# Expert rows turned by transposing DMAs as 16-bit halves, in place of TensorE transposes

## The chip, the cores and the metric

The kernel runs on one core of one Trainium2 chip. The metric is the device time of one execution in microseconds (us), as the median of several runs. The engines are called PE or TensorE (matmuls; PEld is its weight load), DVE or VectorE, ACT or ScalarE, POOL or GpSimd, and SP, which here only issues DMAs. DMAs that SP issues go through hardware queue q1, the gathers that GpSimd issues go through software queue q0; both are served by the same 16 DMA engines.

## The reference

Two layers of "cross attention" and feed-forward work on `x` of shape [4, 512, 512], 2048 tokens of 512 numbers in all. Each part adds its result to `x`:

```python
x = x + L0_xattn(ctx, layernorm(x))   # a state-space scan
x = x + L0_ffn(layernorm(x))          # mixture of 64 experts, 8 for each token
x = x + L1_xattn(layernorm(x), ctx)   # 16 heads of attention
x = x + L1_ffn(layernorm(x))          # two ternary matrix products with GELU between
```

The change lies in the second part, the mixture of experts:

```python
# the gate chooses 8 of 64 experts for each token; rare choices are rerouted
flat_e = rerouted.reshape(-1)
order = jnp.argsort(flat_e)
tok = order // TOP_K
xs = x[tok]                                         # rows sorted by expert
gu = ragged_dot(xs, swapaxes(gate_up_proj, 1, 2), group_sizes)   # [rows, 2*192]
gate, up = split(gu, 2)
y = ragged_dot(silu(gate) * up, swapaxes(down_proj, 1, 2), group_sizes)
out = zeros_like(x).at[tok].add(y * w[:, None])
```

So each expert takes some 230 to 350 normalised rows of 512 float32 numbers, multiplies them with a [512, 384] matrix, and the result with a [192, 512] matrix.

## The kernel before

The kernel goes through four stages in order: the scan (to about 510 us), the gate and the routing (to about 640), the experts (to about 1338), and attention with the last feed-forward (to the end). In the first three stages and in attention the instructions of each engine stand in the order in which the code issues them, so what is issued earlier on an engine or on a DMA queue also runs earlier there.

**The gate.** `Gate.norm(t)` normalises tile t (128 tokens) on ScalarE into a `g_xn` buffer (three of them, pool `r_p3`) and SP stores it to the DRAM table `xn_dram`. TensorE turns the same tile (`turn`), ScalarE copies it (`take`), and TensorE makes the logits for two tiles at a time. `exps` lets GpSimd fill the last columns of `g_z` with constants (two memsets for each tile) and `top` finds the eight best on VectorE. The order of these calls is written out in `route`; norms run four and five tiles ahead. GpSimd also computes the statistics (`Stats.pair`, lines 154 to 157) and issues loads for later keys (lines 864 to 873). The routing then makes, for each expert, a list of its tokens (`tok`).

**The experts.** `Experts.run_in` loops over i from 0 to 65. In iteration i:

- GpSimd issues indirect gathers: the rows of expert i+2 (`xg`, up to three tiles of at most 128 rows) and its weights (`wg`, 6144 bytes a partition; `wd`, 4096 bytes a partition). Buffers come from pool `e_w` with four of each name.
- For m = 0, 1, 2: TensorE does `gate_up` of expert i-1 for the m-th block of 128 outputs (`pg`, line 1314), ScalarE and VectorE make `sg` and `h` of it, and then `turn_x` turns tile m of expert i: four TensorE transposes into the PSUM tile `pt` (line 1298) and one copy to `xT` (line 1301; VectorE for tile 1, ScalarE for the others).
- TensorE does `down` of expert i-2 (`po`, lines 1338 to 1348), ScalarE and VectorE copy the result to `yo`, and SP stores it to `y_dram`.
- Side tasks of the routing and of the later feed-forward (`Ternary.tasks`) are done after that by a quota; the latter load 32 blocks of 512 KB (`wf`) through SP and reduce or round them. They fall mostly on experts 30 to 53.

`xT` has two buffers, `pg` and `po` three each. ROOM fixes how many rows each of the 64 places has, from 352 down to 232; the first 40 have three tiles, the rest two. An expert with more rows than its place would leave rows to a loop in `rest`, which runs only if there are any.

**A transposing DMA elsewhere.** In the attention stage the kernel already turns 2-byte matrices with `nc.sync.dma_start_transpose` (line 2018): `Th<-hq`, 128 by 1024 bf16, and `Tx<-xq`, 128 by 512.

Of the kernel before, what the change touches and what calls it, by code (L numbers as in the profile page):

```python
# [17 lines left out]
F32 = mybir.dt.float32  # L18
F16 = mybir.dt.float16
BF16 = mybir.dt.bfloat16  # L20
I16 = mybir.dt.int16
# [8 lines left out]
P = 128  # L30
B, S, DM = 4, 512, 512
NT = B * S // P
NC = DM // P
# [4 lines left out]
E, TOPK, SEL, FI = 64, 8, 4, 192  # L38
# [12 lines left out]
ROOM = [next(m for m, end in ROOMS if i < end) for i in range(E)]  # L51
BASE = [2 * i + min(i, THREE) for i in range(E + 1)]
# [107 lines left out]
class Gate:  # L160
# [16 lines left out]
    def norm(self, t):  # L177
        nc = self.nc
        n, i = divmod(t, 2)
        xn = self.s[t] = self.rows.tile([P, DM], F32, name="g_xn")  # L180
        nc.scalar.activation(xn, self.x_all[:, t, :], AF.Identity,
                             bias=self.stats.nmr[n][:, i:i + 1],
                             scale=self.stats.rstd[n][:, i:i + 1])
        nc.sync.dma_start(self.dr["xn"][t * P:(t + 1) * P, :], xn)

    def turn(self, t):
        xn = self.s[t]
# [997 lines left out]
class Keys:  # L1185
# [14 lines left out]
    def load(self, h0, h1, pool, tag, queue=None):  # L1200

        t = pool.tile([P, self.KC, (h1 - h0) * HD], F32, name="k_w", tag=tag)
        for h in range(h0, h1, HG):
            cols = slice(h * HD, min(h + HG, h1) * HD)
            (queue or self.nc.sync).dma_start(t[:, :, cols.start - h0 * HD:cols.stop - h0 * HD],
                                   self.w["Wk"][:, cols].rearrange("(k p) e -> p k e", p=P))
        for h in range(h0, h1):
            self.wk[h] = t[:, :, (h - h0) * HD:(h - h0 + 1) * HD]
# [40 lines left out]
        self.pss = None  # L1249


def gather(nc, pool, name, width, table, index):
    n = index.shape[0]
    t = pool.tile([P, width], F32, name=name)
    nc.gpsimd.indirect_dma_start(out=t[0:n, :], out_offset=None, in_=table,  # L1255
                                 in_offset=bass.IndirectOffsetOnAxis(ap=index, axis=0))
    return t


class Expert:  # L1260
# [3 lines left out]
    def __init__(self, cm, wp, sp, yp, ps, pg, po, w, xn_dram):  # L1264
        self.cm, self.nc = cm, cm.nc
        self.wp, self.sp, self.yp, self.ps, self.pg, self.po = wp, sp, yp, ps, pg, po
        self.w, self.xn_dram = w, xn_dram

    def load(self, widx, toks):
        s = {}  # L1270
        self.load_rows(s, toks)
        self.load_weights(s, widx)
        return s

    def load_rows(self, s, toks):

        s["n"] = [t.shape[0] for t in toks]
        s["xg"] = [gather(self.nc, self.wp, f"xg{min(j, 1)}", DM, self.xn_dram[:, :], t)
                   for j, t in enumerate(toks)]

    def load_weights(self, s, widx):
# [6 lines left out]
    def turn_x(self, s, j):  # L1288

        nc = self.nc  # L1290
        if j >= len(s["n"]):
            return
        if j == 0:
            s["xT"] = self.sp.tile([P, NC, 3 * P], F32, name="xT")
        n = s["n"][j]
        pt = self.ps.tile([P, NC, P], F32, name="pt")
        for c in range(NC):
            nc.tensor.transpose(pt[:, c, 0:n], s["xg"][j][0:n, c * P:(c + 1) * P],  # L1298
                                self.cm.ident[0:n, 0:n])
        out = s["xT"][:, :, j * P:j * P + n]  # L1300
        (nc.vector.tensor_copy if j == 1 else nc.scalar.copy)(out, pt[:, :, 0:n])  # L1301

    def gate_up(self, s, m):

# [58 lines left out]
class Experts:  # L1363
# [11 lines left out]

    def load_rows(self, i):
        if i < E:
            self.ex.load_rows(self.st[i], [
                self.r["tok"][0:min(P, ROOM[i] - j * P), j, i:i + 1]
                for j in range(BASE[i + 1] - BASE[i])])  # L1380

    def run(self, tern, more, late, keys, kv):

# [4 lines left out]
    def run_in(self, ctx, tern, more, late, keys, kv):  # L1388
        cm, ex, st = self.cm, self.ex, self.st
        tc = cm.tc  # L1390
        ex.sp = ctx.enter_context(tc.tile_pool(name="e_s", bufs=2))
        ex.yp = ctx.enter_context(tc.tile_pool(name="e_y", bufs=3))
        ex.ps = ctx.enter_context(tc.tile_pool(name="e_ps", bufs=2, space=PSUM))
        ex.pg = ctx.enter_context(tc.tile_pool(name="e_pg", bufs=3, space=PSUM))
        ex.po = ctx.enter_context(tc.tile_pool(name="e_po", bufs=3, space=PSUM))
        tp = ctx.enter_context(tc.tile_pool(name="e_t", bufs=2))
        ctx_k = late_contexts(keys, self.w, late)
        slots, norms = slot_tasks(cm, self.dr, kv, self.r, more, ex.ps)
        tasks = slots + tern.tasks(tp, ex.ps) + norms
        many = len(tasks)  # L1400
        done = 0
        held = []
        QUOTA = 54
        self.load_rows(0)
        self.load_rows(1)
        for i in range(E + 2):
            self.load_rows(i + 2)
            self.load_weights(i + 2)
            for m in range(3):
                if 1 <= i <= E:  # L1410
                    ex.gate_up(st[i - 1], m)
                if m == 0 and held:
                    held.pop()()
                if i < E:
                    ex.turn_x(st[i], m)
            if i >= 2:
                ends = list(range(ROWS[i - 2], ROWS[i - 1], P)) + [ROWS[i - 1]]
                ex.down(st[i - 2], [self.y_dram[r0:r1, :] for r0, r1 in zip(ends, ends[1:])])
                while tasks and not held and done < (i - 1) * many / QUOTA:
                    left = tasks.pop(0)()  # L1420
                    done += 1
                    if left is not None:
                        held.append(left)
        assert not tasks and not held
        return ctx_k


def late_contexts(keys, w, late):

    ctx = {}  # L1430
    for b, tag in ((2, "Th"), (3, "hq")):
        ctx[b] = late.tile([P, CTX // P, S], F32, name="k_ctx", tag=tag)
        keys.nc.sync.dma_start(ctx[b], w["ctxT"][:, b * S:(b + 1) * S].rearrange(
            "(k p) s -> p k s", p=P))
    return ctx


def slot_tasks(cm, dr, kv, r, pool, ps):
# [127 lines left out]
    def key_norms(step):  # L1566
# [9 lines left out]
        else:  # L1576
# [6 lines left out]
            for c0, c1 in cols:  # L1583
# [15 lines left out]
def rest(ctx, cm, x_all, w, xn_dram, z_dram, r, many):  # L1599


    tc, nc = cm.tc, cm.nc
# [18 lines left out]
    tok = cp.tile([P, NOV], I32, name="o_tok")  # L1621
    widx = cp.tile([P, NOV], I32, name="o_widx")
    with tc.tile_pool(name="o_ps", bufs=1, space=PSUM) as ps:
        ends = []
        for name, op in (("before", ALU.is_gt), ("upto", ALU.is_ge)):
            m = cp.tile([E, E], F32, name=f"o_{name}")
# [87 lines left out]
    wp = ctx.enter_context(tc.tile_pool(name="o_w", bufs=1))  # L1714
    ps = ctx.enter_context(tc.tile_pool(name="o_eps", bufs=1, space=PSUM))
    pg = ctx.enter_context(tc.tile_pool(name="o_pg", bufs=3, space=PSUM))
    ex = Expert(cm, wp, wp, wp, ps, pg, ps, w, xn_dram)
    with tc.For_i(0, many, 1) as i:
        at = wp.tile([P, 2], I32, name="o_at")
        vec.tensor_copy(at[:, 0:1], tok[:, bass.ds(i, 1)])  # L1720
        vec.tensor_copy(at[:, 1:2], widx[:, bass.ds(i, 1)])
        s = ex.load(at[:, 1:2], [at[:, 0:1]])
        ex.turn_x(s, 0)
        for m in range(3):
            ex.gate_up(s, m)
        ex.down(s, [z_dram[bass.ds(i * P, P), :]])
# [684 lines left out]
```

## Time and profile before

| What | us |
|---|---|
| median of 3 runs | 2589.12 (2588.2 to 2590.96) |
| the profiled execution | 2588.76 |
| its span | 2587.0 |
| experts, first `pg` matmul to first `pg` matmul of the last expert | 648.5 to 1323.5 |

| Engine | busy us (share of the span) | instructions |
|---|---|---|
| TensorE | 2452.8 (95%) | 9831 |
| VectorE | 1494.9 (58%) | 2565 |
| ScalarE | 1206.2 (47%) | 2323 |
| GpSimd | 1178.2 (46%) | 1108 |

The span is the time from the first to the last instruction of one profiled execution, and the durations of instructions are from that execution. A busy time is the union of the instructions of an engine. The DMA share is the sum of the packets' times over the time of 16 engines; it can go a little over 1, since packets of different queues overlap on an engine. A row of a wait names who waited, for whom, how long in total, how many times, and the longest one.

### The profile page before, as it was taken

Reading aid. Unit: us, or ns where it says so; the run is one execution under the profiler, and the core shown is the slowest. Engines: PE = TensorE matmul, PEld = TensorE weight load, DVE = VectorE, ACT = ScalarE, POOL = GpSimd, SP = SyncE. Lnnn points to the kernel's source line nnn. Section 1 sums busy time; section 2 is a strip of 40 time slices with the busy share of each in tenths; the row PEclk is TensorE's granted clock in tenths of the full one; section 3 lists DMA queues with packets and bytes.
Section 4 is the critical chain, followed back from the end, with each engine's and each line's share of the span. In section 5 each row is a group of like instructions: output and inputs, shape, how many; then the busy total and the mean of one; then the engine's idle time right before and its main releaser. Section 6 shows DMA issues by size and latency. Waiting matters only on the chain. (4 is left out here: it accounts for less than half of the span.)

```text
span 2587.0 us, 29356 instructions
## 1 busy us (share of the span) xinstructions
PE 2452.8 (95%) x9831; PEld 1380.1 (53%) x9831; DVE 1494.9 (58%) x2565; ACT 1206.2 (47%) x2323; POOL 1178.2 (46%) x1108
## 2 busy tenths in 40 slices
PE   6989899988999999999998999999999999999997
PEld 3555555645556566666664444445454454555543
DVE  6999998945332433444225555466665666554546
ACT  6777777655222222333223543454454445554543
POOL 7999999921443444444325333134423343121112
PEclk8999999988999999999998999999999999999999
DMA  5362535343776667899755543233433443332210
GB/s 203 95 223 89 200 127 187 103 150 113 229 221 203 217 219 258 278 334 342 232 177 189 183 130 104 80 122 110 121 104 105 134 144 100 96 96 64 69 41 21
DMA packets 226781, 401.90 MB, mean 155 GB/s; under 512 B 62163, under 2 KB 103203, under 8 KB 222528
## 3 DMA queue, kind: packets, MB, share of 16 engines
q1 hardware_dynamic: 183166, 243.57, 28.8%
q0 software_dynamic: 41408, 156.20, 19.3%
q8 instruction: 81, 1.33, 0.2%
q10 hardware_dynamic: 2050, 0.18, 0.1%
q14 instruction: 76, 0.62, 0.1%
HBM read 312.18 MB, written 79.82 MB: 152 GB/s over the span
## 5 line engine op out<-in xcount | busy, mean ns | idle before, releaser
L1956 DVE TENSOR_REDUCE mx<-psc 128x1 f32<-128x512 f32 x256 | 176.5, 690 | 408.1 <-PE psc L1953 407.9
L1314 PE MATMUL pg<-xT,wg 128*128 128x284 f32 (+12 forms) x1536 | 394.4, 400 | 1.2 <-ACT xT L1301 1.1
L1959 ACT ACTIVATE e<-psc,mx 128x512 f32<-128x512 f32 x256 | 176.0, 688 | 326.9 <-DVE mx L1956 326.3
L1314 PEld LDWEIGHTS pg<-xT,wg 128*128 128x128 f32 x1536 | 278.9, 191 | 91.1 <-issue 40.2
L492 POOL TENSOR_TENSOR dBu<-bb,du 128x1024 f32<-128x1024 f32 x128 | 303.1, 2389 | 4.7 <-DVE dA L517 3.2
L1255 POOL DMA_INDIRECT xg<-xn_dram,tok x168 | 173.0, 1030 | 203.7 <-PE pt L1298 146.3
L1953 PE MATMUL psc<-kT,qT 128*128 128x512 f32 x512 | 261.7, 593 | 0.0
L1980 PE MATMUL po<-eT,v 128*128 128x512 f32 x512 | 231.6, 595 | 9.3 <-ACT eT L1974 9.3
L1919 PE MATMUL pq<-Wq,xnT 128*128 128x512 f32 x512 | 233.5, 599 | 6.3 <-DMA Wq<-Wq 6.3
L1989 PE MATMUL px<-Wo,oT 128*128 128x512 f32 x512 | 231.9, 596 | 0.0
L1973 PEld LDWEIGHTS pet<-ident,e 128*128 128x128 f32 x1024 | 126.3, 141 | 146.6 <-issue 129.6
L1930 POOL TENSOR_SCALAR qms<-qms 128x4 f32<-128x4 f32 x64 | 24.9, 389 | 389.0 <-DVE qms L1928 388.1
L503 ACT ACTIVATE dA<-delta,negA 128x512 f32<-128x512 f32 x256 | 176.3, 694 | 53.8 <-DVE hc L518 35.0
L517 DVE TENSOR_TENSOR_SCAN dA<-dA,dBu 128x1024 f32<-128x1024 f32 x80 | 186.5, 2331 | 16.3 <-ACT dA L503 6.6
L1980 PEld LDWEIGHTS po<-eT,v 128*128 128x128 f32 x512 | 96.1, 190 | 136.1 <-issue 114.8
L1973 PE MATMUL pet<-ident,e 128*128 128x128 f32 x1024 | 154.8, 274 | 6.5 <-DVE e L1965 6.2
L1359 DVE COPY yo<-po 128x512 f32<-128x512 f32 x68 | 46.9, 690 | 196.4 <-PE po L1348 196.4
L523 PEld LDWEIGHTS yT<-ident,hc 128*128 128x128 f32 x1024 | 118.6, 143 | 77.9 <-issue 45.4
L1965 DVE TENSOR_SCALAR e<-e,tot 128x512 f32<-128x512 f32 x256 | 152.8, 597 | 9.1
L523 PE MATMUL yT<-ident,hc 128*128 128x128 f32 x1024 | 132.6, 277 | 21.0 <-DVE yg L557 9.8
L1974 ACT COPY eT<-pet 128x512 f32<-128x512 f32 x256 | 148.0, 578 | 3.2 <-PE pet L1973 2.8
L1919 PEld LDWEIGHTS pq<-Wq,xnT 128*128 128x128 f32 x512 | 93.7, 192 | 101.8 <-issue 95.4
(359 smaller groups left out, 4260.4 us busy)
## 6 DMA issues: line engine op xcount, KB each, us to landing
y_dram<-yo SPq DMA_DIRECT2D x110, 256.0 KB
bb<-bc_dram SPq DMA_DIRECT2D x16, 1024.0 KB
cb<-bc_dram SPq DMA_DIRECT2D x16, 1024.0 KB
v_dram<-v SPq DMA_DIRECT2D x64, 256.0 KB
k_dram<-k_kT SPq DMA_DIRECT2D x64, 256.0 KB
Wq<-Wq SPq DMA_DIRECT2D x16, 1024.0 KB
kT<-k_dram SPq DMA_DIRECT2D x64, 256.0 KB
rk<-r_dram SPq DMA_DIRECT2D x64, 256.0 KB
```

Of the source, the lines that this page charges most:

```text
L492: nc.gpsimd.tensor_tensor(dBus[q], st[b]["bb"][i // 2][:, j:j + 2, :], st[b]["du"][c].unsqueeze(1).to_broadcast([P, 2, S]), ALU.mult)
L503: nc.scalar.activation(dAs[q][:, j, :], st[b]["delta"][c], AF.Exp, scale=negA[:, c, n:n + 1])
L517: nc.vector.tensor_tensor_scan(*flat, 0.0, ALU.mult, ALU.add)
L523: nc.tensor.matmul(yT[:, lc, :], t[:, lc * P:(lc + 1) * P], cm.ident, is_transpose=True, start=first and lc == 0, stop=last, skip_group_ch ...
L1314: nc.tensor.matmul(pg[:, 0:n], s["wg"][:, c, m * P:(m + 1) * P], s["xT"][:, c, 0:n], start=c == 0, stop=c == NC - 1)
L1919: nc.tensor.matmul(pq.rearrange("p h d -> p (h d)"), xnTs[b * NC + i][:, c, :], s["Wq"][:, c, :], start=c == 0, stop=c == NC - 1)
L1953: nc.tensor.matmul(pscore, st[b, g]["qT"][:, h, i * P:(i + 1) * P], ks[n], start=True, stop=True)
L1956: nc.vector.tensor_reduce(mx, pscore, AX.X, ALU.max, negate=True)
L1959: nc.scalar.activation(e, pscore, AF.Exp, bias=mx, accum_out=tot)
L1973: nc.tensor.transpose(pt[:, kc, :], e[:, kc * P:(kc + 1) * P], cm.ident)
L1980: nc.tensor.matmul(po, v[:, kc, :], eT[:, kc, :], start=kc == 0, stop=kc == KB - 1)
L1989: nc.tensor.matmul(px, oTs[j * HG + h][:, i * P:(i + 1) * P], st[b, g]["Wo"][:, h, :], start=h == 0, stop=h == HG - 1)
```

## The change

The gate no longer stores a row as 512 float32 numbers. GpSimd splits each number into its low and its high 16 bits (two copies for each tile of 128 tokens) and the row is stored as 512 low halves followed by 512 high halves; the table has the same number of bytes. The gathers fetch those rows into buffers of a pool of their own (`e_x`, two of each of three names), with the number of rows rounded up to a multiple of 16.

Behind the gather, `turn_rows` issues on SP one transposing DMA for each tile, [rows x 1024] to `xt` [128 x 8 x rows] in 16-bit elements; there is one `xt` buffer for each tile number (`e_xt`). Tile m of expert i+1 is turned in iteration i. `join_x` then puts the halves together: VectorE copies the high halves and ScalarE the low ones into every second 16-bit place of `xT`, which is float32 again. `gate_up` and `down` are as before. The loop in `rest` joins the halves first and turns on TensorE as before.

```diff
@@ Gate.norm
-        nc.sync.dma_start(self.dr["xn"][t * P:(t + 1) * P, :], xn)
+        halves = xn[:, :].bitcast(I16).rearrange("p (d two) -> p two d", two=2)
+        t2 = self.work.tile([P, 2, DM], I16, name="g_halves")
+        for k in range(2):
+            nc.gpsimd.tensor_copy(t2[:, k], halves[:, k])
+        nc.sync.dma_start(self.dr["xn"][t * P:(t + 1) * P, :], t2.rearrange("p k d -> p (k d)"))
@@ Expert
+    def load_rows(self, s, toks, n):
+
+        s["n"] = n
+        s["xg"] = [gather(self.nc, self.xp, f"xg{j}", 2 * DM, self.xn_dram[:, :], t, I16)
                    for j, t in enumerate(toks)]
...
+    def turn_rows(self, s, j):
+
+        if j >= len(s["n"]):
+            return
+        n = -(-s["n"][j] // 16) * 16
+        t = self.tp.tile([P, 2 * NC, n], I16, name=f"xt{j}",
+                         padded_shape=[P, 2 * NC, P if j < 2 else 3 * P // 4])
+        self.nc.sync.dma_start_transpose(t, s["xg"][j][0:n, :])
+        s["xt", j] = t
+
+    def join_x(self, s, j):
 
         nc = self.nc
         if j >= len(s["n"]):
             return
         if j == 0:
             s["xT"] = self.sp.tile([P, NC, 3 * P], F32, name="xT")
-        n = s["n"][j]
+        n, t = s["n"][j], s.pop(("xt", j))
+        out = s["xT"][:, :, :].bitcast(I16).rearrange("p c (t two) -> p two c t", two=2)
+        at = slice(j * P, j * P + n)
+        nc.vector.tensor_copy(out[:, 1, :, at], t[:, NC:, 0:n])
+        nc.scalar.copy(out[:, 0, :, at], t[:, 0:NC, 0:n])
...
-        pt = self.ps.tile([P, NC, P], F32, name="pt")
-        for c in range(NC):
-            nc.tensor.transpose(pt[:, c, 0:n], s["xg"][j][0:n, c * P:(c + 1) * P],
-                                self.cm.ident[0:n, 0:n])
-        out = s["xT"][:, :, j * P:j * P + n]
-        (nc.vector.tensor_copy if j == 1 else nc.scalar.copy)(out, pt[:, :, 0:n])
@@ Experts.run_in
+        ex.xp = ctx.enter_context(tc.tile_pool(name="e_x", bufs=2))
+        ex.tp = ctx.enter_context(tc.tile_pool(name="e_xt", bufs=1))
...
         self.load_rows(0)
         self.load_rows(1)
+        for j in range(3):
+            self.turn_rows(0, j)
         for i in range(E + 2):
             self.load_rows(i + 2)
             self.load_weights(i + 2)
@@ in the loop over m, behind gate_up of expert i-1
                 if i < E:
-                    ex.turn_x(st[i], m)
+                    ex.join_x(st[i], m)
+                self.turn_rows(i + 1, m)
@@ whole
-    dr = dict(xn=dp.tile([B * S, DM], F32, name="xn_dram"),
+    dr = dict(xn=dp.tile([B * S, 2 * DM], I16, name="xn_dram"),
```

More of the change, by code (lines that the diff above doesn't have):

```diff
@@ L1249, in take, with gather @@
         self.pss = None
-def gather(nc, pool, name, width, table, index):
+def gather(nc, pool, name, width, table, index, dtype=F32):
     n = index.shape[0]
-    t = pool.tile([P, width], F32, name=name)
+    t = pool.tile([P, width], dtype, name=name)
     nc.gpsimd.indirect_dma_start(out=t[0:n, :], out_offset=None, in_=table,
@@ L1266, in __init__ @@
         self.wp, self.sp, self.yp, self.ps, self.pg, self.po = wp, sp, yp, ps, pg, po
-        self.w, self.xn_dram = w, xn_dram
+        self.w, self.xn_dram, self.xp = w, xn_dram, wp
     def load(self, widx, toks):
         s = {}
-        self.load_rows(s, toks)
+        self.load_rows(s, toks, [t.shape[0] for t in toks])
         self.load_weights(s, widx)
         return s
-    def load_rows(self, s, toks):
-        s["n"] = [t.shape[0] for t in toks]
-        s["xg"] = [gather(self.nc, self.wp, f"xg{min(j, 1)}", DM, self.xn_dram[:, :], t)
+    def load_rows(self, s, toks, n):
+        s["n"] = n
+        s["xg"] = [gather(self.nc, self.xp, f"xg{j}", 2 * DM, self.xn_dram[:, :], t, I16)
                    for j, t in enumerate(toks)]
@@ L1286, in load_weights @@
             "p (j h) -> p j h", j=2)
-    def turn_x(self, s, j):
+    def turn_rows(self, s, j):
[7 more added lines that the diff above has]
+    def join_x(self, s, j):
         nc = self.nc
@@ L1294, in turn_x @@
             s["xT"] = self.sp.tile([P, NC, 3 * P], F32, name="xT")
-        n = s["n"][j]
+        n, t = s["n"][j], s.pop(("xt", j))
[3 more added lines that the diff above has]
+        nc.scalar.copy(out[:, 0, :, at], t[:, 0:NC, 0:n])
+    def turn_x(self, s):
+        nc = self.nc
+        s["xT"] = self.sp.tile([P, NC, 3 * P], F32, name="xT")
+        x = self.sp.tile([P, DM], F32, name="xj")
+        out = x[:, :].bitcast(I16).rearrange("p (d two) -> p two d", two=2)
+        for k in range(2):
+            nc.vector.tensor_copy(out[:, k], s["xg"][0][:, k * DM:(k + 1) * DM])
         pt = self.ps.tile([P, NC, P], F32, name="pt")
         for c in range(NC):
-            nc.tensor.transpose(pt[:, c, 0:n], s["xg"][j][0:n, c * P:(c + 1) * P],
-                                self.cm.ident[0:n, 0:n])
-        out = s["xT"][:, :, j * P:j * P + n]
-        (nc.vector.tensor_copy if j == 1 else nc.scalar.copy)(out, pt[:, :, 0:n])
+            nc.tensor.transpose(pt[:, c, :], x[:, c * P:(c + 1) * P], self.cm.ident)
+        nc.scalar.copy(s["xT"][:, :, 0:P], pt)
     def gate_up(self, s, m):
@@ L1377, in load_rows, with turn_rows @@
         if i < E:
-            self.ex.load_rows(self.st[i], [
-                self.r["tok"][0:min(P, ROOM[i] - j * P), j, i:i + 1]
-                for j in range(BASE[i + 1] - BASE[i])])
+            n = [min(P, ROOM[i] - j * P) for j in range(BASE[i + 1] - BASE[i])]
+            self.ex.load_rows(self.st[i], [self.r["tok"][0:-(-m // 16) * 16, j, i:i + 1]
+                                           for j, m in enumerate(n)], n)
+    def turn_rows(self, i, j):
+        if i < E:
+            self.ex.turn_rows(self.st[i], j)
     def run(self, tern, more, late, keys, kv):
@@ L1722, in rest @@
         s = ex.load(at[:, 1:2], [at[:, 0:1]])
-        ex.turn_x(s, 0)
+        ex.turn_x(s)
         for m in range(3):
```

## The prediction

> **What bounds the kernel now.** I began with the page's busy times, then took the expert stage alone: the table by stretches, the timeline of one expert, and the DMA view.
>
> ```profile
> PE 2452.8 (95%) x9831; PEld 1380.1 (53%) x9831; DVE 1494.9 (58%) x2565; ACT 1206.2 (47%) x2323; POOL 1178.2 (46%) x1108
> ```
>
> The table by stretches, for experts 1 to 29, 30 to 39, 40 to 53 and 54 to 62:
>
> ```profile
> core 0: us, PE busy (x) PEld busy (x) DVE busy (x) ACT busy (x) POOL busy (x), PEclk, DMA share, GB/s
> 660.16:1002.42 342.26, 342.26 (x1547) 205.55 (x1547) 129.31 (x258) 87.40 (x205) 150.83 (x148) 1.00 0.68 214
> 1002.42:1111.80 109.38, 108.40 (x521) 67.62 (x519) 43.92 (x71) 32.36 (x74) 46.21 (x47) 1.00 0.87 292
> 1111.80:1238.69 126.89, 126.46 (x573) 88.50 (x571) 56.80 (x91) 43.05 (x83) 56.69 (x56) 1.00 0.97 333
> 1238.69:1323.46 84.77, 79.72 (x364) 57.84 (x362) 21.55 (x41) 23.56 (x50) 27.79 (x29) 0.96 0.66 211
> ```
>
> TensorE fills nearly every microsecond at full clock, so what leaves it is gain. But the last two columns say what comes next: the DMA engines are busy 0.68 of the first stretch and 0.97 of the third, where the weights of the later feed-forward pass through as well (`wf`). The change puts its work there.
>
> One expert of 284 rows in the timeline (first column start, second length):
>
> ```profile
> 902.22 2.18 PE L1314 MATMUL pg<-xT,wg 128*128 128x284 f32 x8
> 904.24 0.60 PE L1298 MATMUL pt<-ident,xg 128*128 128x128 f32 x4
> 904.67 2.08 PE L1314 MATMUL pg<-xT,wg 128*128 128x284 f32 x8
> ...
> 909.03 0.43 PE L1298 MATMUL pt<-ident,xg 28*128 28x28 f32 x4
> 909.40 0.70 PE L1338 MATMUL po<-wd,h 128*128 128x512 f32 x1
> ```
>
> From start to start the transposes take 904.67 - 904.24 = 0.43 us, again 0.43 for the second tile, and 909.40 - 909.03 = 0.37 for the short one: 1.23 us of the 11.25 us until the next expert. An expert of two tiles spends 0.85. (Modelled ends overlap; starts are the safer measure.) The overflow loop in `rest`, which keeps transposes on TensorE, did not run in this trace: 672 `pt` transposes are just 4 for each of the 168 tiles of the 64 experts. Its edit costs nothing here.
>
> **The change, part by part.**
>
> TensorE loses all 672 transposes. That is worth at most 1.25 x 29 = 36 us in the first stretch, 1.23 x 10 = 12, 0.85 x 14 = 12 and 0.8 x 9 = 7: some 67 us.
>
> Their work goes to 168 transposing DMAs on SP, each of a [128 rows x 1024 halves] tile or a part of it. The trace has exactly this operation: `Th<-hq`, 128x1024 in 2-byte elements. The DMA view of one of them alone (1888.4 to 1890.0 us, 40 slices of 0.04 us), then one that was disturbed (1820.1 to 1824.1, slices of 0.1 us):
>
> ```profile
> DMA  0002589999999999999999999999999999742100
> q1 hardware_dynamic: 1056, 0.26, 85.4%
> ...
> DMA  0000000000071799999990000000000599999025
> GB/s 0 0 0 0 0 0 0 0 0 0 0 164 31 151 210 218 192 215 177 69 23 0 0 13 5 10 10 10 8 10 10 118 282 289 287 318 418 20 61 205
> ```
>
> Alone it takes 85.4% of 1.6 us = 1.4 us of all 16 engines, 190 GB/s, in packets under 512 B. Disturbed, everything stands for about 1 us in the middle while only some 10 GB/s trickle, and the tile takes 2.5 us from first packet to last. It looks as if the engines move in step in such a transfer and wait for the slowest. In the expert stage gathers are under way nearly always; no row shows a transpose beside a gather. So a tile costs between 1.4 and 2.7 us; I take 1.8, nearer to the quiet row, because an engine that waits may serve another queue.
>
> What the other transfers need: 214 GB/s x 342.26 us / 29 = 2.53 MB an expert, then 3.19, 3.02 and 1.99 MB. The fastest five microseconds of this stage moved
>
> ```profile
> 1214.00:1219.00 5.00, 5.00 (x27) 4.17 (x26) 1.45 (x2) 1.73 (x3) 2.75 (x3) 1.00 1.04 401
> ```
>
> 401 GB/s, so those are 6.3, 8.0, 7.5 and 5.0 us an expert. An expert has 2.25, 2.125, 2 and 1.9 tiles. The period is the larger of TensorE's new time and the DMA sum (us an expert):
>
> - experts 1 to 29: before 11.80, TensorE after 10.55; DMA 6.3 + 4.05 = 10.35. Gain 1.25 x 29 = 36.
> - 30 to 39: before 10.94, TensorE 9.71; DMA 8.0 + 3.8 = 11.8. Loss 9.
> - 40 to 53: before 9.06, TensorE 8.2; DMA 7.5 + 3.6 = 11.1. Loss 2.04 x 14 = 29.
> - 54 to 62: before 8.6 (a stall of 7 us at one of them left aside), TensorE 7.8; DMA 8.4. Gain 2.
>
> Sum: 0. At 1.4 us a tile DMA needs 9.45, 11.0, 10.3 and 7.6: -36, +1, +17, -7 = -25 us. At 2.7 us, 12.4, 13.7, 12.9 and 10.1: +17, +28, +54, +14 = +113.
>
> Here the Trainium skill speaks for the change: "Advanced Engine Details and Errata", section "X-Bar Transpose (TRN2)", expects a transposing DMA at 350 to 400 GB/s, as fast as a copy. Then a tile of 262 kB is about 0.7 us, TensorE stays the bound nearly everywhere, and the sum is -36 -12 -2 -7 = -57. The row says 1.4, half that rate; the row decides. Another rule speaks against: "VectorE: DVE Perf Modes", section "The three transpose paths", gives 1309 ns for one 128x128 block by DMA and advises TensorE where PSUM will do. Eight such blocks one after another would be 10.5 us a tile, over 20 us an expert; the row has eight in 1.4, so as a rate it does not hold.
>
> Waits on SP. `turn_rows(i+1, m)` waits for its gather and for both joins of expert i (one `xt` buffer each). Behind it stand the `y_dram` stores and the `wf` loads. An issue takes 1.24 us (`Th` group): 3 x 1.24 plus the four stores (903.04 to 905.89, 2.85 us) is 6.6 of 10 us, and SP waited 529 us for `yo` before; no cost while landings come within about 8 us, which is when the next expert's join wants the tile. POOL's row gathers, which waited 146 us for TensorE, now wait for a transpose that landed an iteration earlier: hidden.
>
> Joins: ScalarE copied 104 tiles out of PSUM (583 ns), VectorE 64 (692). Now both copy half of all 168; nearest row the 128x512 VectorE pass at 597 ns. Both engines are at most 45% busy in every stretch, and a joined tile is first used an iteration later: cost 0, unless the tile lands late; then the joins hold up `sg` and `h` behind them.
>
> The gate stage. `norm` gets two GpSimd copies a tile and its store waits for them. Rows:
>
> ```profile
> L1804 POOL TENSOR_SCALAR hq<-hid 128x512 bf16<-128x512 f32 x64 | 44.0, 705 | 166.0 <-DVE hid L1803 166.0
> ...
> 530.07 0.23 POOL L157 TENSOR_SCALAR s_all<-s_all 128x2 f32<-128x2 f32 x1
> 530.23 0.10 POOL L219 MEMSET g_z<- 128x4 f32 x1
> ...
> DVE g_z L230 <- POOL g_z L219: 4.7, 2, 4.1
> ```
>
> GpSimd is late already: VectorE waits 4.1 us for that first memset. In the order of instructions the copies of tiles 0 to 4 come between L157 and it: 10 x 0.7 = 7 us, and about 2 us because two `g_halves` buffers wait for stores to land. ScalarE's fourth normalisation, at 518.9, also waits for a `g_xn` buffer that GpSimd reads only after 530. Later the copies fit (2.8 us in a pair's 7). Cost 9 us, all on the path to the first gather; 5 if a copy takes 0.35 us, 14 at the 1.28 of a two-operand pass.
>
> The start of the stage. SP first issues the two `k_ctx` loads, then the transposes of expert 0:
>
> ```profile
> 645.13 3.58 SPq L1433 DMA_DIRECT2D k_ctx<-ctxT  x2
> ...
> 648.53 5.06 PE L1314 MATMUL pg<-xT,wg 128*128 128x352 f32 x8 [0.57 <-ACT xT L1301]
> ```
>
> 1 MB at the 250 to 290 GB/s of these microseconds is 4 us in the same queue, then three transposes (5) and a join (0.6): near 657 in place of 648.5. Cost 8 us (4 to 14).
>
> Sum: 0 + 9 + 8 = +17 us. The profiled execution took 2588.8 us (span 2587.0), 0.4 below the median of the runs, 2589.1; so 2589 + 17 = 2606 us. A measurement here can tell about 0.2%, 5 us, from no change.
>
> **Rivals.**
>
> 1. Transposes are cheap beside gathers (quiet row or the skill's rate). For: the dense stretch already ran at 97% without stalling TensorE. Against: the disturbed row. Time: -25 + 17 = -8, to -57 + 17 = -40: 2581 to 2549, less if the gate costs only 5. This is the faster side; it decides where a tile costs under 1.5 us.
> 2. Transposes in step hold all engines (2.7 us a tile): +113 + 17, 2719. For: the disturbed row; gathers have packets of 4 and 6 KB. Against: it was seen with other traffic in the same queue only.
> 3. Landing latency: with one buffer each, turn, landing and join form a ring; over 8 us, joins hold ScalarE and SP. One more microsecond in each of the 33 experts of the later stretches: +33 on the sum, 2639. SP's long waits for `yo` speak against it in the first stretch.
>
> That the change doesn't do what it says is unlikely: the order of instructions has no `pt` transposes for the 64 experts and 168 DMAs instead.
>
> **How the numbers follow.** The sum as taken (2590 to 2640): 0.38. Rival 1: 0.31. Rival 2: 0.12. Rival 3: 0.12. Within 5 us by cancellation: 0.07. The range 2562 to 2690 leaves out the far halves of rivals 1 and 2. Faster 0.31, same 0.08, slower 0.61.
>
> **What would show it.** Right: by stretch, periods near 10.5 in experts 16 to 23 (before 11.25) but over 10 in 40 to 53 (before 9.0), with DMA share near 1 and ScalarE or VectorE waiting for `xt`; the first `g_z` memset 9 us later; the first `pg` matmul 8 us later relative to its first gather. Wrong: TensorE still without gaps in 40 to 53 (rival 1), or periods over 11.5 already in the first stretch (rival 2).

## The result, and the profile after

The changed kernel takes 2788.3 us (median of four runs, 2782.97 to 2817.36) where the kernel before, on the same chip, takes 2588.66 (2584.45 to 2590.96): a ratio of 1.0796 with a 95% interval of 1.0720 to 1.0872, 200 us slower. The prediction said 2606, with a range to 2690.

The profiled execution took 2782.97 us (span 2781.3), against 2588.76 (2587.0) before: 194 us more. The page's line of busy times:

```profile
PE 2438.8 (88%) x9159; PEld 1363.4 (49%) x9159; DVE 1519.6 (55%) x2669; ACT 1269.3 (46%) x2387; POOL 1187.4 (43%) x1140
```

TensorE issues the 672 transposes less, as planned (9159 matmuls for 9831), yet its busy time falls by only 14 us, and its share from 95% to 88%. The table by stretches shows where; these are the same experts as in the prediction's table (1 to 29, 30 to 39, 40 to 53, 54 to 62):

```profile
core 0: us, PE busy (x) PEld busy (x) DVE busy (x) ACT busy (x) POOL busy (x), PEclk, DMA share, GB/s
682.65:1042.52 359.87, 320.02 (x1199) 187.19 (x1199) 140.51 (x316) 116.14 (x234) 143.39 (x146) 0.94 1.11 250
1042.52:1206.91 164.39, 110.26 (x402) 67.81 (x402) 47.01 (x90) 42.02 (x84) 44.34 (x48) 0.82 1.11 227
1206.91:1404.28 197.37, 135.24 (x458) 92.72 (x458) 59.56 (x106) 56.29 (x98) 54.31 (x56) 0.81 1.12 250
1404.28:1511.79 107.51, 79.65 (x291) 56.77 (x291) 23.65 (x51) 31.40 (x60) 29.33 (x31) 0.84 1.07 226
```

The stretches are 17.6, 55.0, 70.5 and 22.7 us longer than before, 166 us together. In each, two columns contradict each other: the DMA share is over 1, but the bytes moved are 226 to 250 GB/s, where the same engines moved 292 and 333 GB/s in the second and third stretch before. Something keeps the DMA engines occupied without moving data. TensorE's granted clock (PEclk) fell too, from 1.00 to 0.81 in the third stretch.

Who waits for it, from the waits of the changed kernel (who waited, for whom, us in total, times, longest):

```profile
POOL xg L1259 <- DMA xt<-xg: 450.3, 95, 18.2
DVE xT L1312 <- DMA xt<-xg: 311.5, 85, 17.0
ACT xT L1313 <- DMA xt<-xg: 307.1, 90, 17.0
PE pg L1339 <- ACT xT L1313: 171.4, 33, 13.8
ACT yo L1384 <- DMA y_dram<-yo: 68.3, 31, 5.0
```

Line 1299 is now the transposing DMA (`xt<-xg`), 1312 and 1313 the two joins, 1339 `gate_up`, 1384 a copy to `yo`. TensorE's share of these waits is the row with 171 us, behind ScalarE's join, which in turn waits for the turned tile.

One stall, from the timeline (start, length, engine):

```profile
1172.12 8.59 SPq L1299 DMA_TRANSPOSE xt<-xg  x2
...
1187.33 0.76 ACT L1313 COPY xT<-xt 128x512 int16<-128x512 int16 x1 [6.06 <-DMA xt<-xg]
...
1189.30 0.41 ACT L1350 COPY h<-h 64x264 f32<-64x264 f32 x1
...
1190.10 8.41 PE L1339 MATMUL pg<-xT,wg 128*128 128x264 f32 x24 [6.79 <-ACT h L1350]
```

SP needs 8.59 us to issue two transposing DMAs (over the whole kernel the median of one issue is 1.93 us and the longest 13.52; the fields are min, median and max in ns):

```profile
L1299 SPq DMA_TRANSPOSE xt<-xg x168: 846/1926/13520, 656.0 to 1501.2; - x168
```

The tile lands at 1187.33; ScalarE sat 6.06 us ahead of its join, with `sg` and `h` of the expert before queued behind it, and TensorE stood 6.79 us. The DMA view of 1174 to 1184 us (40 slices of 0.25 us; a packet counts wholly in the slice in which it starts) shows what the DMA engines did while the two were issued and just after:

```profile
DMA  8799799990100019999969979934459123899999
GB/s 328 301 278 229 287 133 197 88 52 0 16 0 16 17 20 51 176 86 90 114 73 349 156 79 198 102 71 84 77 70 135 69 90 153 244 306 310 360 356 364
```

From 1176.25 to 1177.75 the view is dark: hardly a packet starts and 0 to 20 GB/s flow. The engines are not idle then: the packet records have 21 packets under way at 1177.0. Some of those that began before and do not end, as a plain table:

```
start us   took ns   bytes   queue      end us
1174.68      3066      256   q1        1177.75
1174.98      2760      256   q1        1177.74
1175.25      2496      256   q1        1177.75
1175.77      1982      256   q1        1177.75
1175.92      1838     4096   q0        1177.76
```

In all, 17 packets of transposing DMAs, four of them shown, stand there; they start between 1173.40 and 1175.90. Twelve end within 40 ns of 1177.76 and the other five within 15 ns of 1177.94. A packet of 256 bytes otherwise takes 18 ns (the median). They look as if they waited for one another. A packet of q0 that started behind them ends with them; but three others of q0 begin and end while they stand, and two end 0.5 us later, so q0 is slowed rather than shut.

The dark spell is only a part of this wait. From 1182.5 to 1186.5 the packets of q0 that start carry 1.12 MB, some 280 GB/s, and only 412 packets of transposing DMAs start beside them; in the last microsecond, when q0 is nearly empty, 597 do. So the tile also waited while the engines moved other data.

Over the whole expert stage the transposing DMAs have 4089 packets longer than 200 ns: 3% of their packets and 38% of their time, and three quarters of these (75%) end within 20 ns of at least three others of them. Were each end moved at random by up to 1 us, 4% would.

### The profile page after: what moved, and what is told of

Same layout as the page of the kernel before. It is cut to its first block, busy times and chain, and to the rows that moved or that the text cites. A ratio compares the mean times of both kernels' runs of the same rounds, so it can differ in the third digit from the quotient of the medians.

```text
span 2781.3 us, 28648 instructions
## 1 busy us (share of the span) xinstructions
PE 2438.8 (88%) x9159; PEld 1363.4 (49%) x9159; DVE 1519.6 (55%) x2669; ACT 1269.3 (46%) x2387; POOL 1187.4 (43%) x1140
## 5 line engine op out<-in xcount | busy, mean ns | idle before, releaser
L1339 PE MATMUL pg<-xT,wg 128*128 128x284 f32 (+12 forms) x1536 | 435.5, 447 | 197.8 <-ACT xT L1313 171.4
L1339 PEld LDWEIGHTS pg<-xT,wg 128*128 128x128 f32 x1536 | 329.9, 219 | 318.8 <-ACT xT L1313 184.9
L1259 POOL DMA_INDIRECT xg<-xn_dram,tok x168 | 162.7, 968 | 509.7 <-DMA xt<-xg 450.3
L1313 ACT COPY xT<-xt 128x512 int16<-128x512 int16 (+3 forms) x168 | 110.4, 657 | 311.2 <-DMA xt<-xg 307.1
L1312 DVE COPY xT<-xt 128x512 int16<-128x512 int16 (+3 forms) x168 | 68.6, 408 | 314.6 <-DMA xt<-xg 311.5
```

The source lines that it names most:

```text
L1339: nc.tensor.matmul(pg[:, 0:n], s["wg"][:, c, m * P:(m + 1) * P], s["xT"][:, c, 0:n], start=c == 0, stop=c == NC - 1)
```

## The experiments

Three theories stand against each other. **A, held in step:** a transposing DMA needs all 16 engines together, so that it and whatever runs beside it hold each other up, and the engines lose capacity. **B, the ring:** the DMA engines are well, and the chain of turn, landing and join through single `xt` buffers costs the time. **C, the bytes:** 37 MB more in 256-byte pieces are simply too much, transposed or not. The table gathers what the packet records say of each (expert stage, first `pg` of expert 0 to first `pg` of expert 63; packet means in ns; the 256-byte packets are those of the transposing or copying DMA; "engine time" is the sum of the packets' times over 16 engines, in us).

| Kernel | median us | ratio to before (95%) | stage us | 256 B, mean | 256 B, engine time | gathers of 4 and 6 KB, engine time |
|---|---|---|---|---|---|---|
| before | 2588.66 | | 674.9 | | | 364 |
| after | 2788.3 | 1.0796 (1.0720 to 1.0872) | 847.0 | 37 | 324 | 451 |
| 1 before + unused turns | 2738.31 | 1.0593 (1.0529 to 1.0658) | 825.8 | 35 | 314 | 418 |
| 2 before + unused plain copies | 2611.44 | 1.0114 (1.0069 to 1.0158) | 697.8 | 20 | 182 | 358 |
| 3 after, joins don't wait | 2808.12 | 1.0863 (1.0795 to 1.0931) | 887.0 | 39 | 346 | 463 |
| 4 after, plain copies | 2588.72 | 1.0018 (0.9992 to 1.0045) | 654.1 | 20 | 181 | 338 |
| 5 after, no weight gathers | 2564.5 | 0.9915 (0.9880 to 0.9951) | 636.9 | 27 | 241 | 163 |
| 6 after, weights in q1 | 2676.38 | 1.0356 (1.0324 to 1.0388) | 744.7 | 28 | 241 | 377 |
| 7 gate alone, join late | 2923.38 | 1.1311 (1.1260 to 1.1362) | 995.7 | | | 377 |
| 8 gate alone, join ahead | 2601.88 | 1.0045 (1.0024 to 1.0066) | 676.5 | | | 352 |
| 9 after, DMAs kept apart | 2733.96 | 1.0552 (1.0511 to 1.0592) | 794.3 | 26 | 225 | 328 |
| 10 before + a third of the turns | 2659.56 | 1.0264 (1.0176 to 1.0353) | 728.5 | 38 | 161 | 388 |
| 11 as 1, stores by ScalarE | 2847.32 | 1.0993 (1.0926 to 1.1061) | 938.2 | 39 | 346 | 443 |
| 12 after, stores by ScalarE | 2820.44 | 1.0889 (1.0831 to 1.0948) | 889.8 | 42 | 367 | 424 |

(The "gathers" of 6 are its weight loads in q1, with the `wf` packets of 4 KB among them, and the row gathers in q0; those of 5 are without most weights. A packet's time includes what it waits for others, so a column is occupation, not work.)

**1. The DMAs without the rest of the change.** To the kernel before, behind `turn_x`:

```diff
                     ex.turn_x(st[i], m)
+                self.unused(i + 1, m)   # dma_start_transpose(xt, xg as int16), nobody reads xt
```

> The kernel before, with TensorE's transposes and float32 rows as they were, plus the 168 transposing DMAs of the change at the same places of SP's queue, into xt buffers that nobody reads (and the row gathers in the change's two-buffer pool). The gate is untouched. Three theories of the 200 us. A (held in step): a transposing DMA needs all 16 DMA engines together, so it and the gathers beside it hold each other up, and gathers and stores come late whoever waits for the turned tile: 2700 to 2780. B (ring): what costs is the chain turn, landing, join with single xt buffers, in which ScalarE, VectorE and SP wait; nobody waits here, so 2590 to 2620. C (bytes): the 37 MB more in 256-byte pieces fill the engines, transposed or not: as A, 2700 to 2780.

Measured: 2738.31, 155 us above the runs of before beside it (2583.63). No join waits for a tile here and TensorE still has its own transposes, so B in the form of the joins' waits falls as the main cause. (The gathers still wait until a transposing DMA has read their buffer; run 2 has the same buffers.) What waits is ScalarE, for the stores to free `yo`, and the gathers:

```profile
ACT yo L1359 <- DMA y_dram<-yo: 230.2, 29, 15.7
POOL xg L1255 <- DMA xt<-xg: 224.1, 46, 16.0
```

The loss is not spread evenly: experts 16 to 29 kept the 11.25 and 11.07 us of before exactly, experts 1 to 15 went from 12.4 to 15.2 us each and 40 to 53 from 9.1 to 14.5. In experts 16 to 29 the packets are held too (a mean of 29 ns in 16 to 23 and of 36 in 24 to 29, with a DMA share of 1.07 and 1.11), with weight gathers beside them, and it costs no time. So neither a held packet nor a share over 1 is a loss by itself; it is one where TensorE runs out of work.

**2. The same bytes, plainly copied.** The rows are not turned, and nobody reads them.

```diff
-        self.cm.nc.sync.dma_start_transpose(t, x)
+        self.cm.nc.sync.dma_start(t[0:n, :, 0:P], x.rearrange("p (c k) -> p c k", c=2 * NC))
```

> As the run before it, but each of the 168 unused DMAs is a plain copy of the same bytes from xg to xt, in pieces of 256 bytes like the transposing one, rows not turned. A: a plain copy needs no step, so 2590 to 2630. B: 2590 to 2620. C: the same bytes in the same pieces, so as long as with transposing DMAs, 2700 to 2780.

Measured: 2611.44, 28 us above before, against 155. The packets have the same size and number; they take a mean of 20 ns, and not one of 144640 took over 200. So of the 155 us some 28 belong to the bytes (C, a part of it) and 127 to the transposing (A).

**3. The ring without its wait.** The joins copy a constant, so this kernel leaves out the rows.

```diff
-        nc.vector.tensor_copy(out[:, 1, :, at], t[:, NC:, 0:n])
-        nc.scalar.copy(out[:, 0, :, at], t[:, 0:NC, 0:n])
+        nc.vector.tensor_copy(out[:, 1, :, at], constant)
+        nc.scalar.copy(out[:, 0, :, at], constant)
```

> The changed kernel with its transposing DMAs, but join_x copies one constant into xT instead of the halves in xt, so that no engine waits for a turned tile to land; only the next transposing DMA into the same buffer does. A: gathers and SP's queue are still held up, 2720 to 2780. B: most of the 172 us of the expert stage come back, 2600 to 2640. C: 2720 to 2780.

Measured: 2808.12. Nothing comes back, the stage is even 40 us longer than in the changed kernel. So the joins' 311 and 307 us of waiting are where the loss shows, not what makes it. One thing did move: from the first row gather to the first `pg` it took 7.1 us, where the changed kernel takes 18.8.

**4. The ring with a plain copy in it.** The rows reach the joins, but not turned.

```diff
-        self.nc.sync.dma_start_transpose(t, s["xg"][j][0:n, :])
+        self.nc.sync.dma_start(t[0:n], s["xg"][j][0:n, :].rearrange("p (c k) -> p c k", c=2 * NC))
```

> The changed kernel with the whole ring as it is (single xt buffers, joins that wait), but the DMA between xg and xt is a plain copy in 256-byte pieces in place of a transposing one; rows are not turned. A: the loss in the expert stage goes, and TensorE is without its transposes: 2540 to 2620. B: the ring is the same, 2740 to 2790. C: 2740 to 2790.

Measured: 2588.72, as fast as before (0.9992 to 1.0045). All 200 us go when the DMA no longer transposes, with ring, joins, gate and queue order untouched. That the DMA transposes is the cause; how it does the harm, in step as A has it, this run does not show. SP's issue of one such DMA also falls, to a median of 0.61 us. The stretches of this kernel, for the same experts:

```profile
679.49:983.97 304.48, 302.97 (x1199) 176.59 (x1199) 139.21 (x316) 113.97 (x234) 151.72 (x145) 0.99 1.04 302
983.97:1092.35 108.38, 98.20 (x405) 60.10 (x403) 46.45 (x90) 41.81 (x84) 43.61 (x46) 0.97 1.04 330
1092.35:1236.44 144.09, 124.79 (x458) 84.92 (x458) 59.74 (x106) 55.55 (x98) 53.59 (x56) 0.92 1.06 347
1236.44:1322.50 86.06, 74.23 (x291) 52.90 (x291) 23.91 (x51) 31.30 (x60) 29.29 (x31) 0.92 0.94 272
```

A DMA share over 1 here goes with 302 to 347 GB/s. Against before, the stretches change by -37.8, -1.0, +17.2 and +1.3 us.

**5. Less to collide with.** From the fifth expert on, weights of the first four are used again, so this kernel leaves out 60 experts' weight gathers:

```diff
+                s["wg"], s["wd"] = self.st[i % 4]["wg"], self.st[i % 4]["wd"]
```

> The changed kernel without the weight gathers from the fifth expert on (the weights of the first four are used again), so that transposing DMAs meet only row gathers, stores and the later layer's weight loads. A: with little to hold them up, 256-byte packets fall from a mean of 37 ns towards the 20 ns of a plain copy, TensorE is the bound in experts 16 to 29 (about 9.8 us each, as with plain copies), and the kernel takes 2530 to 2600. Were a transposing DMA slow by itself (fixed 2.3 us a tile), the mean stays near 37 ns.

Measured: 2564.5. Experts 16 to 23, which meet only row gathers and stores, are bound by TensorE (9.82 us each, against 11.25 before and 12.19 in the changed kernel), and their transposing packets have means of 21 to 24 ns. SP's issue has a median of 1.24 us, as in the quiet stage. The table by stretches for them:

```profile
855.00:934.00 79.00, 79.00 (x323) 46.73 (x322) 39.97 (x70) 30.51 (x65) 23.30 (x26) 1.00 0.72 181
```

TensorE fills all 79 us, with the transposing DMAs under way. From expert 30 on, where the later layer's `wf` loads pass, stalls come back (14.66 us at expert 35, 12.45 at 49). So a transposing DMA isn't slow by itself; it becomes slow in company (which, as run 1 shows, need not cost time).

**6. The company moved to the same queue.** The loads take their weights at fixed places, and not those that the routing chose; the bytes are the same.

```diff
+                self.cm.nc.sync.dma_start(wg, self.w["gate_up"][i * P:(i + 1) * P, :])
+                self.cm.nc.sync.dma_start(wd, self.w["down"][i * P:(i + 1) * P, :])
```

> The changed kernel with the weights of experts 5 to 64 as plain loads at fixed places, issued by SP into q1 in front of the transposing DMAs: the same bytes and packet sizes, but in the queue of the transposing DMAs in place of the software queue q0. If what hurts is the meeting of two queues on an engine (A, narrow form), 256-byte packets take about 20 ns and the kernel 2540 to 2640. If any traffic beside a transposing DMA hurts (A, wide form), or plain bytes (C), it stays at 2700 to 2800.

Measured: 2676.38, between the two expectations. Over half of the loss goes when the weights stand in one queue with the transposing DMAs, and the mean falls from 37 to 28 ns. The rest stays, with row gathers still in q0. What remains is close to full engines: the packets' times of the five largest kinds sum to 734 us of the stage's 744.7. So the meeting of queues may be a large part of it, though not all. The run does not show it alone: it also puts the weights ahead of the transposing DMAs in one line and takes the issue of 120 gathers from GpSimd.

**7 and 8. The gate's part alone.** No transposing DMAs; the halves are joined into a row-major tile and TensorE turns it.

```diff
+        x = self.sp.tile([P, DM], F32, name="xj")
+        nc.vector.tensor_copy(out[0:n, 1], t[0:n, DM:])
+        nc.scalar.copy(out[0:n, 0], t[0:n, 0:DM])
+        for c in range(NC):
+            nc.tensor.transpose(pt[:, c, 0:n], x[0:n, c * P:(c + 1) * P],
+                                self.cm.ident[0:n, 0:n])
```

> The changed kernel without its transposing DMAs: rows are split in the gate and gathered as halves as in the change, then joined by VectorE and ScalarE into a row-major tile and turned by TensorE as before. All theories: the gate's 7 us, a slower first join, and little in the expert stage, 2592 to 2615.

Measured: 2923.38, a miss, and an error in the order: the join stands directly ahead of its transposes, and in the queues of ScalarE and VectorE behind `sg` and `h`. TensorE paid for it:

```profile
PE pt L1315 <- DVE xj L1311: 183.9, 121, 8.5
PE pt L1315 <- ACT xj L1312: 79.2, 44, 6.1
```

In the next kernel the joins come one iteration ahead, where the change issues its transposing DMAs (`turn_rows` does the joins of expert i+1, `join_x` the transposes of expert i).

> The gate part alone, once more: no transposing DMAs; rows split in the gate, gathered as halves, joined by VectorE and ScalarE one iteration ahead into row-major tiles (as early as the transposing DMAs were issued), then turned by TensorE as before. In the first try the join stood directly ahead of the transposes and TensorE waited for it. All theories: the 7 us of the gate and perhaps a few more, 2588 to 2602.

Measured: 2601.88, 11.7 us above the runs of before beside it, at the upper end of what was expected; the stage is 1.6 us longer than before. The gate is a small cost, and next to nothing of the 172 us.

**9. Kept apart in time.** GpSimd writes one element of each `xt` buffer from the next expert's weights (so the transposing DMA waits until they have landed), and reads one element of each turned tile ahead of the next weight gathers:

```diff
+                    cm.nc.gpsimd.tensor_copy(st[i + 1]["xt", m][0:1, 0, 0:1],
+                                             st[i + 1]["w%s" % "gd"[m % 2]][0:1, 0, 0:1])
...
+                    cm.nc.gpsimd.tensor_copy(ex.seen[0:1, m:m + 1],
+                                             st[i + 1]["xt", m][0:1, 0, 0:1])
+            self.load_weights(i + 2)
```

> The changed kernel, with transposing DMAs and weight gathers kept apart from the third expert on: GpSimd touches the xt buffers only when the next expert's weights have landed, so transposing DMAs start after them, and it reads the turned tiles before it issues the next weight gathers. A (they hold each other up): 256-byte packets fall from a mean of 37 ns to 20 to 24, weight packets from 399 and 249 to about the 285 and 219 of before; the time depends on what the waiting costs, 2620 to 2780. If a transposing DMA were slow for another reason, the means stay and the time rises above 2800.

Measured: 2733.96. This kernel adds waits, and takes none away (it also issues the weight gathers later in the iteration), and it is 54 us faster than the changed one. The same bytes take less of the engines. The queues' shares in the four stretches together, first for the changed kernel (829.14 us), then for this one (783.16 us); columns are packets, MB and share of 16 engines:

```profile
q1 hardware_dynamic: 170026, 86.68, 56.9%
q0 software_dynamic: 28581, 113.84, 53.7%
```

```profile
q1 hardware_dynamic: 170748, 86.77, 48.9%
q0 software_dynamic: 28785, 114.48, 41.7%
```

That is 0.569 x 829.14 = 472 us of the engines for q1 against 383, and 445 against 327 for q0. The mean of 256-byte packets falls to 26 ns, that of the 6-KB weight packets from 399 to 287 (285 before). The expectation named 20 to 24 ns; stores, row gathers and `wf` loads were not kept apart. What is left of the loss was not split; the joins wait even longer for turned tiles than in the changed kernel (VectorE 385.5 us, ScalarE 365.9).

**10. A third of the DMAs.** As run 1, only for the first tile of each expert:

```diff
-        if i >= E or j >= len(self.st[i]["n"]):
+        if i >= E or j >= 1:
```

> The kernel before with unused transposing DMAs as in the first run, but only for the first tile of each expert, 64 in place of 168. If each transposing DMA costs its share: 155 x 64/168 = 59 us, 2640. If the loss begins only when the DMA engines are full (demand): 2584 to 2605, and only experts 40 to 53 grow.

Measured: 2659.56 (two runs, 2641.67 and 2677.46), 51 to 87 us above the 2590.2 of before: too much for a loss that begins only with full engines, and the two runs are too far apart to test the 59 us of a share by number. The place is clearer, in the profiled run of 2641.67: experts 2 to 29 kept their old periods, and of the 53.6 us by which the stage grew, 35 lie in experts 40 to 53 and 15 in 30 to 39. There the DMA engines were 0.97 and 0.87 busy before.

**11 and 12. The stores out of SP's line.** In run 1 and in the changed kernel:

```diff
-                nc.sync.dma_start(out, yo[0:m, :])
+                nc.scalar.dma_start(out, yo[0:m, :])
```

> The kernel before with the 168 unused transposing DMAs (the first run), but the stores of yo issued by ScalarE instead of SP, so that they stand in no line behind transposing DMAs. It asks by which path the held-up DMAs reach TensorE where nobody waits for a turned tile. If through SP's queue (yo stores issued late, then yo buffers, ScalarE and VectorE): most of the 155 us go, 2600 to 2640. If through late gathers or late landing of the stores themselves: 2690 to 2740.

> The changed kernel with the stores of yo issued by ScalarE instead of SP. If SP's queue is the path: 2640 to 2720. If the turned tiles themselves land late because the DMA engines are held up (A): the joins wait as before, 2760 to 2810.

Measured: 2847.32 and 2820.44, both slower still: by 109 us against run 1, far outside what was expected, and by 32 against the changed kernel, where the intervals overlap. So taking the stores out of SP's line does not bring the loss back. That SP's line costs nothing is not shown, since the change has costs of its own: the stores now come through a third queue, q10, and packets of all kinds are held longer: the 256-byte ones 39 and 42 ns, the `wf` loads' 4-KB ones 222 and 218 ns where run 1 and the changed kernel had 181 and 173. ScalarE now also issues DMAs, which run 11 cannot tell from the third queue as a cause of its large loss.

No run beats the kernel before with all of its work done. By run 4, a transposing DMA at the price of a plain copy would only break even (an estimate, since its rows are not turned).

## Why the prediction was wrong

**The direction held, the size did not.** The chance of slower was given as 0.61, but the number put on it was 17 us, and it was 200. Rival 2 ("transposes in step hold all engines") comes nearest to what the runs show, and its own sum, 2719, was too small as well.

**The step that failed is the price of a tile.** The prediction bounded it by two rows, 1.4 us alone and 2.7 us disturbed, and took 1.8 "because an engine that waits may serve another queue". The stall above shows little of that: q0 let three packets through in 1.5 us, and another ended only with the transposing packets. In the changed kernel a full tile (1024 packets) costs 64 x 37 ns = 2.4 us of 16 engines by its own packets. To that comes what it does to others: gathers occupy 451 us where they occupied 338 beside plain copies (run 4), 113 us over about 137 full tiles, 0.8 us each. Together 3.2 us, above the upper bound. The two rows had also been read in different measures: the quiet one by the time that the packets took (85.4% of 1.6 us), the disturbed one from first packet to last. By the packets' time the disturbed window has

```profile
q1 hardware_dynamic: 1092, 0.34, 85.3%
```

that is 85.3% of 4.0 us = 3.4 us, of which the packet records give the tile 3.0. And no row showed what the neighbours lose.

The prediction named a sign for rival 2, periods over 11.5 us in the first stretch, and for its own sum 10.5 in experts 16 to 23. Measured: 359.87 / 29 = 12.4 us, and 12.2.

**The formula was good for plain copies, and not tested for transposes.** Put 3.2 into the prediction's own sum: experts 1 to 29 need 6.3 + 2.25 x 3.2 = 13.5 us, 30 to 39 14.8, 40 to 53 13.9, 54 to 62 11.1; minus the old periods (9.42 in the last stretch, with its one stall) that is +49, +39, +68 and +15, 171 us, and the four stretches grew by 166 (the first less than that, 18, and the second more, 55). The price is fitted to this run, and a packet's time includes its waiting, which cost nothing in run 1's experts 16 to 29; so 3.2 us is what a tile occupies, and no fixed price. A real test is run 4, whose tiles cost 64 x 20 ns = 1.3 us: the prediction's line for 1.4 us reads -36, +1, +17, -7 us, and run 4 measured -37.8, -1.0, +17.2 and +1.3: the first three agree. TensorE's gain of 1.25 us an expert is also right, if a little small: 302.97 us busy in the first stretch for 342.26 is 1.35.

**Two terms on the path to the tile were put at nothing.** An issue on SP was taken at 1.24 us; it had a median of 1.93 and at most 13.52, where run 9, which keeps the DMAs apart, has 1.24 and 3.31. And the row gathers' wait for the transposing DMA was called hidden: it was 450 us, where they had waited 146 us for TensorE. What each is worth alone, no run shows.

**The gate and the start.** Both terms held. The first exponential of `exps` on ScalarE moved from 525.3 to 534.1 us, 8.8 for 9 (the first `g_z` memset, the sign that was named, from 530.2 to 538.3, 8.1). The first row gather moved from 638.9 to 646.0 us, 7.1 for 9 predicted, since a GpSimd copy takes 617 ns where 700 was taken. From that gather to the first `pg` it was 18.8 us for 9.6, 9.2 more for 8 predicted. Run 3, whose joins don't wait, needed 7.1 us for it, so it is the wait for turned tiles.

**Landing latency (rival 3)**, as a wait of the joins, was not the cause: run 3 has no such wait and is no faster.

**The skill's rule.** The Trainium skill, "Advanced Engine Details and Errata", section "X-Bar Transpose (TRN2)", gives transposing DMAs as about as fast as copies. With few neighbours this case agrees (22 ns a packet in run 5's experts 16 to 23, 20 in a plain copy of the same pieces), at half the 350 to 400 GB/s that it states: 16 x 256 bytes in 22 ns is 186 GB/s, an estimate that takes one packet at a time on each engine. Beside the traffic of the changed kernel it does not hold: 37 ns, 111 GB/s.

**A cost that the prediction left out: TensorE's clock behind a stall.** The stall shown above, and the 14 us around it by stretches:

```profile
1184.00:1190.00 6.00, 0.00 (x0) 0.00 (x0) 1.86 (x6) 2.54 (x5) 1.64 (x2) 0.63 1.09 323
1190.00:1196.00 6.00, 5.90 (x14) 4.64 (x15) 3.91 (x7) 3.33 (x6) 2.59 (x3) 0.51 1.11 237
1196.00:1198.30 2.30, 2.30 (x12) 1.98 (x11) 0.80 (x2) 1.05 (x2) 0.95 (x1) 1.00 1.68 114
```

TensorE idles 6.79 us, comes back at half clock (0.51) for 6 us, and then has 1.00. Its 24 `pg` matmuls take 8.41 us where the same block of 264 rows takes about 6 before. The Trainium skill, "TensorE: Matmul & The Clock Gate", section "What's actually happening", says that the clock halves after an idle window of about 3.4 us and returns after about 3.4 us of sustained work; the row shows nearer to 6. The changed kernel has 26 gaps of over 3 us in the stage, where before had one. TensorE is busy 645 us in its four stretches (the column "PE busy" summed) and 600 in run 4, with the same instructions: 45 us more. The clock accounts for them: 128 us of its busy time were at half clock, in run 4 40, and weighted by the clock the two come to 581 and 580 us. That consumed most of the 57 us that its transposes had cost (656.8 before, less 600). In the gaps themselves it lost 192 us over the whole stage.

What stays open: that packets of transposing DMAs wait for one another is read from their common end; what makes them wait, no run shows. And why experts 1 to 15 lose much in runs 1 and 3 and little in the changed kernel, and 16 to 29 lose nothing in run 1, with the same DMAs at about the same places, was not found.

## What to carry to other kernels

A transposing DMA was cheap here where the DMA engines had little else to do (1.4 us for a full tile). Beside gathers and loads it and they held each other up, and where TensorE then ran out of work, both sides paid; before you move transposes from TensorE to DMA, look for stretches where the DMA share is low and no gather is under way. Price such a step by what it takes from its neighbours, not only by its own row, and read a quiet and a disturbed row in the same measure. And read DMA share beside GB/s: a share near 1 with falling GB/s is waiting, not work. And a TensorE that starves pays a second time with its clock, as behind the gap of 6.8 us above.

## What the runs showed of the hardware that was not expected

- Packets of transposing DMAs that are held end together: 75% of those over 200 ns end within 20 ns of three others or more. Packets of other queues take longer beside them (6-KB weight packets 399 ns for 285), though few end with them. Of 286136 plain-copy packets of the same size in runs 2 and 4, two took over 200 ns.
- More waiting made the kernel faster: keeping transposing DMAs and weight gathers apart gave 54 us back (run 9, with intervals that don't overlap).
- Stores issued by ScalarE through a third queue, in place of SP's, made it worse: 109 us in run 11, and 32 in run 12, where the intervals overlap.
- The most that plain traffic kept up over one of the four stretches was 347 GB/s (run 4, the third, DMA share 1.06), not the 401 that the fastest five microseconds before had shown.
- Held packets need not cost time: in run 1's experts 16 to 29 the DMA share was 1.07 to 1.11 and the periods stayed exactly as before.
